# Attention block: queries and keys transposed by VectorE with transfers through DRAM, instead of by TensorE

## The chip, the core and the metric

The program runs on one NeuronCore of one Trainium2 chip. Its engines work in parallel, each through its own list of instructions in order: TensorE (PE, matrix products; PEld is its weight load), VectorE (DVE), ScalarE (ACT), GpSimd (POOL) and SyncE (SP), which here only issues transfers (DMA). TensorE writes into PSUM, eight banks of 128 x 512 fp32 words; everything else lies in SBUF. The metric is device time in microseconds (us) of one execution, lower being better. Where several runs were taken, their median is given.

## The reference

All data are fp32. One transformer block with its layernorms behind the additions:

```python
x = layernorm(x + attn(x));  x = layernorm(x + ffn(x))     # x: (2, 512, 512)

def attn(x):                       # 32 query heads, 8 key/value heads, 128 wide
    q = rmsnorm(heads(x @ Wq.T), q_norm_w)
    k = rmsnorm(heads(x @ Wk.T), k_norm_w)
    v = heads(x @ Wv.T)
    scores = einsum('bkgqd,bksd->bkgqs', grouped(q), k) / sqrt(128)
    bias = where(rel > 0, -1e30, slopes * rel)   # causal, ALiBi: one slope per query head
    return merge(softmax(scores + bias) @ v) @ Wo.T

def ffn(x):                        # inner width 1376, integer weights with a scale per row
    return ((silu(x @ gate.T * gs) * (x @ up.T * us)) @ down.T) * ds
```

`rmsnorm` divides each head's 128 numbers by their root mean square and multiplies by a weight of 128 numbers.

## The kernel before

**Order of the work.** The kernel doesn't issue instructions as it describes them. `Work.add` records each operation with what it reads and writes, a priority and a cost estimate per engine that could run it. `emit` then goes through a planned time: of all operations that are ready and have room in their buffers, the one that can start earliest goes next, ties by priority. The result is one fixed instruction list per engine. Where two engines are allowed (ScalarE or VectorE for an eviction, say), the plan also chooses. Buffers come from rings (`Ring`): so many slots each, taken when the first operation on a buffer is placed, free again when its last one is planned to have ended.

**Attention.** There are 8 groups (a key/value head with its 4 query heads), 2 batches and 4 blocks of 128 tokens: 64 units (g, b, i), run two at a time as 32 pairs. Groups 0 to 5 go through both batches in turn; the last two groups go through batch 0 and then batch 1, so (7, 1) is the last group and batch. For each pair:

- `project` (L759) makes q, k and v of both blocks with a Strassen-like scheme of seven products (`seven`, L605, its matmuls at L617) into `c`, a ring of 2 slots. The first pair uses plain products (L733).
- `heads` (L827) squares q and k (ScalarE, L842), sums (VectorE, L851), takes the power -1/2 (GpSimd, L544) and multiplies into `sq` (L558), a single buffer. GpSimd or ScalarE copies v out of `c` into `v`, and half a block of it into `vs` (L892 to L911). Then TensorE transposes the four query heads of each block into the PSUM bank `ptq` (L920), and an eviction with the weight as its scale brings them to `qT` (L928 on ScalarE, L930 on VectorE), a ring of 2. The keys of both blocks go the same way through `ptk` (L943) to `kT` (L950, L952). Both use the one slot of the PSUM ring `pt`.
- `scores` (L964): 4 matmuls per unit, each of 32 tokens x 4 heads against up to 512 keys (L979). VectorE adds the bias and takes the maximum (L988), ScalarE takes the exponential with its sum (L1004), and ScalarE or GpSimd divides (L1036, L1038), giving the probabilities `pr`.
- `attend` (L1050): every block of 128 keys of `pr` is turned without TensorE. VectorE transposes 32 x 32 squares into `st` (L1072). SyncE stores `st` to `far` in DRAM (L1081), and two loads bring it back in the wanted order as `prT` (L1092). Then TensorE multiplies with v (L1115) and an eviction gives `aT`. `st` and `prT` share a ring of 8 slots. Units 1 and 3 take half a block more along; what is left over for two units is done in one go (`halves`, L1143).
- For groups 0 to 5 `project_out` (L1215) multiplies with Wo by two levels of seven products (`inner`, L1327, matmuls at L1338); groups 6 and 7 use `project_pair` (L1296). VectorE adds everything into `acc`.

Weights for the next group are loaded beside the work: `w` (L402) and `wo` (L449), a ring of 1, whose load waits until the old one has been used.

**The rest.** Layernorm (`norm1`, L1477), the feed-forward part (`ffn_up`, L1631; `ffn_down`, L1795) and the last layernorm with the stores. It runs from some 760 us on.

**Queues.** All transfers but six go through SyncE's queue, in the plan's order. An instruction that waits there holds back everything behind it. Each transfer uses one of eight semaphores in turn.

Of the kernel before, what the change touches and what calls it, by code (L numbers as in the profile page):

```python
# [38 lines left out]
MAX_INIT = 3e38  # L39
DEEP = HKV - 2  # L40
# [15 lines left out]
def act(n, scaled=False):  # L56
    return 0.15 + 0.00084 * n + (0.1 if scaled else 0.0)
# [18 lines left out]
class Ring:  # L76
# [12 lines left out]
    def room(self):  # L89

        best = None
        if self.pool is not None:
            for k, b in enumerate(self.slots):
                t = 0.0
                for u in b.users if b else ():
                    if u["end"] is None:
                        break
                    t = max(t, u["end"] + LAG[u["eng"]])
                else:
                    if best is None or t < best[0]:  # L100
                        best = (t, self, k)
        if self.later is not None:
            found = self.later.room()
            if found is not None and (best is None or found[0] < best[0]):
                best = found
        return best
# [21 lines left out]
class Work:  # L128
# [51 lines left out]
    def emit(self):  # L180
# [23 lines left out]
        def room(o):  # L204

            t = o["at"]
            for b in o["takes"]:
                if b.tile is not None:
                    continue
                r = b.ring  # L210
                found = r.room()
                if found is None:
                    return None
                t = max(t, found[0])
            return t
# [56 lines left out]
def post_ln_block(  # L272
# [4 lines left out]

# [31 lines left out]
    def ring(stage, name, bufs, shape, dtype=F32):  # L309
        r = Ring(name, bufs, shape, dtype)  # L310
        rings.setdefault(stage, []).append(r)
        return r
# [6 lines left out]
    r_pt = ring("psum", "pt", 1, [P, S])  # L319
    r_po = ring("psum", "po", 1, [P, S])  # L320
# [6 lines left out]
    r_qw = ring("all", "qw", 1, [P, HKV])  # L327
    r_kw = ring("all", "kw", 1, [P, 1])
# [14 lines left out]
    r_c = ring("qkv", "c", 2, [P, 2, 2, W3])  # L343
# [7 lines left out]
    r_qT = ring("att", "qT", 2, [P, 2, G * Q, 2])  # L351
# [108 lines left out]
    def idle(e):  # L460
# [3 lines left out]
    warm = Buf(r_pt, "warm")  # L464
    W.add({"PE": 2.9}, -9.0, idle, [A(ident)], [A(warm)])
    load_qkv(0, -9.0)
    load(0.01, -8.9, lambda q: q.dma_start(qw[:, 0:1], qnw), [A(qw)])
    load(0.01, -8.9, lambda q: q.dma_start(kw.tile, knw), [A(kw)])
    W.add(
        {"DVE": 0.1},  # L470
        -5.0,
        lambda e: nc.vector.tensor_scalar_mul(kw.tile, kw.tile, math.sqrt(HD)),
        [A(kw)],
        [A(kw)],
    )
# [3 lines left out]
    for g in reversed(range(1, HKV)):  # L479
        W.add(  # L480
            {"DVE": 0.1},
            -5.0,
            lambda e, g=g: nc.vector.tensor_scalar_mul(
                qw[:, g : g + 1], qw[:, 0:1], SHRINK**g
            ),
            [A(qw)],
            [A(qw)],
        )
# [337 lines left out]

    def heads(p, prio):  # L827
# [52 lines left out]
        for r in range(2):  # L880
            tensor(
                5 * HD,
                prio,
                lambda r=r: sq[:, r],
                lambda r=r: c(r)[:, : 5 * HD].rearrange("p (h d) -> p h d", h=G + 1),
                lambda r=r: inv[:, r].unsqueeze(2).to_broadcast([P, G + 1, HD]),
                ALU.mult,
                [(cb, (r, 0)), (cb, (r, 1)), (inv, r)],
                [(sq, r)],
            )  # L890
            copy_op(
                HD,  # L892
                prio + 0.2,
                lambda r=r: v[:, i + r, :],
                lambda r=r: c(r)[:, 5 * HD :],
                [(cb, (r, 1))],
                [(v, i + r)],
                ("ACT", "POOL"),
            )

        v2 = Buf(r_vs, f"vs_{p}")
        v2s[p] = v2
        copy_op(
            HD,
            prio + 0.2,
            lambda: v2[P // 2 :, :],
            lambda: c(0)[: P // 2, 5 * HD :],
            [(cb, (0, 1))],
            [A(v2)],
            ("ACT", "POOL"),  # L910
        )  # L911
        for r in range(2):
            key = f"{g}_{b}_{i + r}"
            pt = Buf(r_pt, f"ptq_{key}")
            qT = Buf(r_qT, f"qT_{key}")
            qTs[g, b, i + r] = qT

            def transposes(e, r=r, pt=pt):
                for h, k in enumerate((0, 1, 3, 4)):
                    nc.tensor.transpose(pt[:, ts(h, P)], sq[:, r, k, :], ident.tile)  # L920

            W.add({"PE": 4 * TR}, prio + 0.4, transposes, [(sq, r), A(ident)], [A(pt)])

            def evict(e, pt=pt, qT=qT):
                src = pt.tile.rearrange("p (h m c) -> p m h c", h=G, m=2)
                dst = qT.tile.rearrange("p m (h r) k -> p m h (r k)", h=G)
                if e == "ACT":
                    nc.scalar.activation(dst, src, AF.Copy, scale=qw[:, g : g + 1])  # L928
                else:
                    nc.vector.tensor_scalar_mul(dst, src, qw[:, g : g + 1])  # L930

            W.add(
                {"ACT": act(S, True), "DVE": dve(S) + 0.05},
                prio + 0.4,
                evict,
                [A(pt), A(qw)],
                [A(qT)],
            )
        ptk = Buf(r_pt, f"ptk_{p}")

        def transposes_k(e):
            for r in range(2):
                nc.tensor.transpose(ptk[:, ts(r, P)], sq[:, r, 2, :], ident.tile)  # L943

        W.add({"PE": 2 * TR}, prio + 0.4, transposes_k, [(sq, 0), (sq, 1), A(ident)], [A(ptk)])
        def evict_k(e):
            dst = kT[:, i * P : (i + 2) * P].rearrange("p (m k r) -> p m k r", m=4, k=2)
            src = ptk[:, : 2 * P].rearrange("p (m r k) -> p m k r", m=4, k=2)
            if e == "ACT":
                nc.scalar.activation(dst, src, AF.Copy, scale=kw.tile)  # L950
            else:
                nc.vector.tensor_scalar_mul(dst, src, kw.tile)  # L952

        W.add(
            {"DVE": 0.48, "ACT": act(2 * P, True)},
            prio + 0.4,
            evict_k,
            [A(ptk), A(kw)],
# [5 lines left out]
    def scores(u, prio):  # L964
# [8 lines left out]
        for a in range(NQ):  # L973
# [6 lines left out]
                    sc[:, :w], lhsT=qT[:, a // 2, :, a % 2], rhs=kT[:, :w], start=True, stop=True  # L980
# [69 lines left out]
    def attend(u, prio):  # L1050
# [9 lines left out]
        for j in range(i + 1):  # L1060
            st, prT = Buf(r_prT, f"st_{key}_{j}"), Buf(r_prT, f"prT_{key}_{j}")
            prTs[u, j] = prT
            a0 = 2 if j == i and r == 0 else 0
            reads = [(pr, a) for a in range(a0, NQ)]
            if j == i and r:
                reads += [(pr, ("x", a)) for a in range(2)]

            n = (NQ - a0) * Q
            far = Buf(r_far, f"far_{key}_{j}")

            def squares(e, j=j, st=st, a0=a0, n=n):
                nc.vector.transpose(  # L1072
                    st[:, : NQ * n].rearrange("p (m a q) -> p a m q", m=NQ, q=Q),
                    pr[:, a0:, ts(j, P)].rearrange("p a (m k) -> p a m k", m=NQ),
                )

            W.add({"DVE": dve(NQ * n)}, prio, squares, reads, [A(st)])
            load(
                0.26 * n / P,
                prio + 0.1,  # L1080
                lambda q, st=st, far=far, n=n: q.dma_start(  # L1081
                    far[: P * NQ * n].rearrange("(m p c) -> p m c", m=2, p=P),
                    st[:, : NQ * n].rearrange("p (m c) -> p m c", m=2),
                ),
                [A(far)],
                [A(st)],
            )
            for m in range(2):
                load(
                    0.13 * n / P,  # L1090
                    prio + 0.1,
                    lambda q, m=m, far=far, prT=prT, n=n: q.dma_start(  # L1092
                        prT[ts(m, H2), : G * n].rearrange("p (h c) -> p h c", h=G),
                        far[m * H2 * NQ * n : (m + 1) * H2 * NQ * n].rearrange(
                            "(h k c) -> k h c", h=G, k=H2
                        ),
                    ),
                    [(prT, m)],
                    [A(far)],
                )  # L1100
# [8 lines left out]
        for j in range(i + 1):  # L1109
# [13 lines left out]
                [(prT, 0), (prT, 1), (v, j)] + ([A(po)] if j else []),  # L1123
# [16 lines left out]
        banks = (Buf(r_pt, f"px_{key}"), Buf(r_po, f"pz_{key}"))  # L1140
# [17 lines left out]
        for q, j in both:  # L1158
            reads += [(prTs[(g, b, j), j], m) for m in range(2)] + [(v, j), A(v2s[q])]
# [317 lines left out]
    def norm1(t, prio):  # L1477
        b, i = divmod(t, NTB)
        layernorm(t, prio, lambda: y_row(t), y_keys(t), f"a{t}")
        pt = Buf(r_pt, f"ptx_{t}")  # L1480
# [314 lines left out]
    def ffn_down(t, prio):  # L1795
# [37 lines left out]
        for r in (0, 1):  # L1833
            bank = Buf(r_pt, f"ps_{t + r}")
# [105 lines left out]
```

## Time and profile before

| | us |
|---|---|
| median of 3 runs | 999.28 (996.18 to 1000.93) |
| profiled execution, its own time | 998.64 |
| span of that execution in the trace | 996.9 |
| granted TensorE clock in it | 0.995 |

| engine | busy us | share of the span | instructions |
|---|---|---|---|
| TensorE, matmuls | 976.9 | 98% | 4538 |
| TensorE, weight loads | 712.9 | 72% | 4538 |
| VectorE | 722.8 | 73% | 1743 |
| GpSimd | 495.9 | 50% | 573 |
| ScalarE | 451.0 | 45% | 1184 |

DMA moved 119.78 MB in 160267 packets. SyncE's queue issued 592 transfers.

How to read it: a matmul of fp32 shows as two records, a transpose as one. Matmuls are pipelined, so one record lasts from its start until its result has come out, and the next one starts before that. What a matmul takes out of TensorE's time is therefore the distance from its start to the next start. Idle time stands in the profile with the instruction that ended the wait. Idle time of an engine that is not the bottleneck costs nothing.

### The profile page before, as it was taken

To read this page: it belongs to the slowest core of one execution; us is meant where nothing else is said; L and a number is where in the kernel's file an instruction comes from. 1 tells how busy PE (TensorE), PEld (TensorE's weight loads), DVE (VectorE), ACT (ScalarE), POOL (GpSimd) and SP (SyncE) were. 2 spreads that over 40 slices of the span, in tenths; PEclk is the share of its full clock that TensorE was granted. 3 is DMA by queue.
4 is the path that set the end of the run, shared out by engine and by line. 5 is a ranking of instruction groups with operands and counts; after the bars stand their busy time and mean duration, and the time that the engine had idled before them with its cause. 6 is when DMAs were issued, how large, how long until landed. Compare 5 with 4: busy or idle time off the path is not lost. (4 is left out here: it accounts for less than half of the span.)

```text
span 996.9 us, 14270 instructions
## 1 busy us (share of the span) xinstructions
PE 976.9 (98%) x4538; PEld 712.9 (72%) x4538; DVE 722.8 (73%) x1743; ACT 451.0 (45%) x1184; POOL 495.9 (50%) x573
## 2 busy tenths in 40 slices
PE   9999999999999999999999999999989999999997
PEld 5566776577767767676767676776747688888886
DVE  7877676877877888778767888776776586668544
ACT  2756354555355545645564445444454333433100
POOL 6774384537444646654567387565434152123120
PEclk9999999999999999999999999999999999999999
DMA  8273336425414634262436263725256443210001
GB/s 313 79 209 112 105 110 183 130 85 159 138 43 148 190 107 126 77 194 91 143 88 208 77 206 94 215 60 149 75 170 172 112 117 85 80 51 22 12 31 43
DMA packets 160267, 119.78 MB, mean 120 GB/s; under 512 B 27488, under 2 KB 151008, under 8 KB 158912
## 3 DMA queue, kind: packets, MB, share of 16 engines
q1 hardware_dynamic: 159328, 118.21, 39.5%
q8 instruction: 36, 0.59, 0.3%
q10 hardware_dynamic: 864, 0.66, 0.2%
q14 instruction: 39, 0.32, 0.1%
HBM read 78.98 MB, written 39.85 MB: 119 GB/s over the span
## 5 line engine op out<-in xcount | busy, mean ns | idle before, releaser
L1004 ACT ACTIVATE pr<-pr,nmax 128x32 f32<-128x32 f32 (+15 forms) x256 | 131.4, 514 | 69.2 <-DVE nmax L988 68.2
L979 PE MATMUL sc<-kT,qT 128*128 128x160 f32 (+15 forms) x512 | 149.6, 405 | 1.5 <-DVE nmax L988 1.4
L1115 PE MATMUL pa<-prT,v 128*128 128x512 f32 (+1 forms) x320 | 139.4, 518 | 5.4 <-DMA prT<-far 5.3
L988 DVE CUSTOM_DVE_ANT_0 pr<-sc,bias 128x32 f32<-128x32 f32 (+15 forms) x256 | 108.4, 434 | 36.5 <-PE sc L979 33.3
L979 PEld LDWEIGHTS sc<-kT,qT 128*128 128x128 f32 x512 | 89.7, 196 | 43.2 <-issue 21.2
L558 DVE TENSOR_TENSOR acc<-acc,pa_o 128x512 f32<-128x512 f32 (+2 forms) x128 | 72.8, 569 | 50.7 <-PE pa_o L1338 33.5
L1072 DVE STREAM_TRANSPOSE st<-pr 128x512 f32<-128x512 f32 (+1 forms) x160 | 96.0, 635 | 3.8 <-ACT pr L1036 2.1
L1036 ACT ACTIVATE pr<-pr,rden 128x64 f32<-128x64 f32 (+12 forms) x204 | 85.5, 481 | 26.5 <-DVE rden L1019 26.1
L617 PE MATMUL pa_q<-tq,sx 128*128 128x384 f32 x248 | 90.8, 489 | 0.0
L1038 POOL TENSOR_SCALAR pr<-pr,rden 128x256 f32<-128x256 f32 (+12 forms) x84 | 41.9, 508 | 75.3 <-DVE rden L1019 74.6
L714 ACT COPY c<-pa_q 128x384 f32<-128x384 f32 x84 | 39.9, 476 | 87.0 <-PE pa_q L617 83.9
L1115 PEld LDWEIGHTS pa<-prT,v 128*128 128x128 f32 x320 | 54.6, 193 | 24.8 <-issue 7.1
L714 ACT COPY gu<-pa_h 128x256 f32<-128x256 f32 (+1 forms) x88 | 32.3, 370 | 76.1 <-PE pa_h L617 62.1
L544 POOL TENSOR_TENSOR inv<-ms,nhalf 128x10 f32<-128x10 f32 (+1 forms) x33 | 64.0, 1939 | 4.3 <-DVE ms L865 2.8
L617 PEld LDWEIGHTS pa_q<-tq,sx 128*128 128x128 f32 x248 | 45.2, 190 | 27.6 <-issue 5.2
L851 DVE TENSOR_REDUCE ms<-sq 128x5 f32<-128x640 f32 x64 | 51.4, 813 | 7.7 <-ACT sq L842 7.7
L928 ACT ACTIVATE qT<-ptq,qw 128x512 f32<-128x512 f32 x50 | 34.3, 687 | 49.8 <-PE ptq L920 49.6
L842 ACT ACTIVATE sq<-c 128x640 f32<-128x640 f32 x64 | 45.6, 731 | 23.6 <-DVE c L558 21.5
L558 POOL TENSOR_TENSOR sq<-c,inv 128x640 f32<-128x640 f32 x42 | 52.7, 1267 | 0.6
L714 ACT COPY aT<-pa 128x512 f32<-128x512 f32 (+1 forms) x48 | 25.1, 522 | 51.4 <-PE pa L1115 50.7
L558 DVE TENSOR_TENSOR c<-pb_q,c 128x384 f32<-128x384 f32 x62 | 34.1, 550 | 19.6 <-PE pb_q L617 14.4
L617 PE MATMUL pa_h<-tx,sw 128*128 128x256 f32 (+1 forms) x176 | 46.1, 386 | 2.2 <-ACT gu L714 2.2
(226 smaller groups left out, 2233.5 us busy)
## 6 DMA issues: line engine op xcount, KB each, us to landing
far<-st SPq DMA_DIRECT2D x128, 256.0 KB, 2.3
prT<-far SPq DMA_DIRECT2D x256, 128.0 KB, 3.0
w<-in_wqkv_dram SPq DMA_DIRECT2D x39, 384.0 KB, 5.1
wo<-in_wot_dram SPq DMA_DIRECT2D x10, 1024.0 KB, 5.1
far<-st SPq DMA_DIRECT2D x32, 128.0 KB, 1.9
prT<-far SPq DMA_DIRECT2D x64, 64.0 KB, 2.4
wi<-in_gwt_dram SPq DMA_DIRECT2D x14, 256.0 KB, 3.0
wi<-in_uwt_dram SPq DMA_DIRECT2D x14, 256.0 KB, 3.4
```

The lines of the kernel that those rows point to most:

```text
L544: lambda e: nc.gpsimd.tensor_tensor(dst(), src(), nhalf[:, :n], ALU.pow),
L558: lambda e: vec[e].tensor_tensor(dst(), a(), b(), alu),
L617: nc.tensor.matmul(bank[:rows, :width], lhsT=a(fa, c), rhs=b(fb, c), start=(fresh and c == 0), stop=(c == depth - 1), skip_group_check=True,)
L714: nc.scalar.copy(dst(), src())
L842: lambda e, r=r: nc.scalar.activation(sq[:, r].rearrange("p h d -> p (h d)"), c(r)[:, : 5 * HD], AF.Square),
L851: lambda e, r=r: nc.vector.tensor_reduce(ms[:, r], sq[:, r], AX.X, ALU.add),
L979: lambda e, a=a, w=w, sc=sc: nc.tensor.matmul(sc[:, :w], lhsT=qT[:, a // 2, :, a % 2], rhs=kT[:, :w], start=True, stop=True),
L988: lambda e, a=a, w=w, sc=sc: nc.vector.tensor_tensor_reduce(out=pr[:, a, :w], in0=sc[:, :w], in1=bias[:, S - w :], scale=-(SHRINK**-g), sc ...
L1004: lambda e, a=a, w=w: nc.scalar.activation(pr[:, a, :w], pr[:, a, :w], AF.Exp, bias=nmax[:, a : a + 1], scale=-1.0, accum_out=den[:, a : a ...
L1036: nc.scalar.activation(dst, src, AF.Copy, scale=rden[:, a : a + 1])
L1072: nc.vector.transpose(st[:, : NQ * n].rearrange("p (m a q) -> p a m q", m=NQ, q=Q), pr[:, a0:, ts(j, P)].rearrange("p a (m k) -> p a m k", ...
L1115: lambda e, j=j, prT=prT, n=n: nc.tensor.matmul(by_head(po.tile)[:, :, P - n // G :], lhsT=v[:, j, :], rhs=late(prT, j, n), start=(j == 0) ...
```

## The change

- `NEAR_Q` and `NEAR_P` name two pairs of group and batch, (0, 0) and (7, 1), "near" from here on; the other 14 are "far".
- Queries and keys of the far ones (28 pairs): VectorE transposes the 32 x 32 squares (`squares`), SyncE stores the result to DRAM (`far_away`) and a load with another order of the blocks brings it back as `qT`, or as `raw` for the keys. The keys are multiplied with the weight on the way to `kT` (`weigh`, ScalarE or GpSimd). In the near ones TensorE transposes as before.
- The probabilities of the near ones go to TensorE: up to four transposes per block into a PSUM bank, and an eviction to `prT`. The far ones are unchanged but for the helper functions.
- v and vs of the far ones: four and two transfers from `c`, straight into the order of rows that the products want, in place of copies by ScalarE and GpSimd.
- The weights of the query norm and of the key norm are multiplied together once per group and applied to the keys alone; queries have no scale any more.
- Rings: `c` 2 to 3, `qT` 2 to 3; the PSUM rings `pt` and `po`, one bank each, become one ring `po` of two. `st` and `raw` of queries and keys come from the ring of `prT`. `room` now counts each slot only once if an operation takes two buffers of one ring.
- Layouts on the host: tokens in their natural order, the heads as q, k, v. `sc` reads `qT[:, a, :]` in place of `qT[:, a // 2, :, a % 2]`.

```diff
+NEAR_Q = {(0, 0), (HKV - 1, 1)}
+NEAR_P = {(0, 0), (HKV - 1, 1)}
...
-    r_pt = ring("psum", "pt", 1, [P, S])
-    r_po = ring("psum", "po", 1, [P, S])
+    r_po = ring("psum", "po", 2, [P, S])
...
-    r_c = ring("qkv", "c", 2, [P, 2, 2, W3])
+    r_c = ring("qkv", "c", 3, [P, 2, 2, W3])
...
-    r_qT = ring("att", "qT", 2, [P, 2, G * Q, 2])
+    r_qT = ring("att", "qT", 3, [P, NQ, P])
...
+    def squares(st, dst, src, n, prio, reads):
+        W.add(
+            {"DVE": dve(n)}, prio, lambda e: nc.vector.transpose(dst(), src()), reads, [A(st)]
+        )
+
+    def far_away(st, n, parts, name, prio):
+        far = Buf(r_far, f"far_{name}")
+        load(
+            0.26 * n / S,
+            prio,
+            lambda q: q.dma_start(
+                far[: P * n].rearrange("(m p c) -> p m c", m=parts, p=P),
+                st[:, :n].rearrange("p (m c) -> p m c", m=parts),
+            ),
+            [A(far)],
+            [A(st)],
+        )
+        return far
...
+        if (g, b) in NEAR_P:
...
+        else:
+            for m in range(NQ):
+                at = H2 * (m // 2) + m % 2
+                load(
+                    0.13 / NQ,
+                    prio + 0.2,
+                    lambda q, m=m, at=at: q.dma_start(
+                        v[at : at + H2 - 1 : 2, i : i + 2, :], cb[ts(m, Q), :, 1, 2 * HD :]
+                    ),
+                    [(v, (i + r, m)) for r in range(2)],
+                    [(cb, (r, 1)) for r in range(2)],
+                )
+            for m in range(2):
+                load(
+                    0.02,
+                    prio + 0.2,
+                    lambda q, m=m: q.dma_start(v2[H2 + m : P : 2, :], cb[ts(m, Q), 0, 1, 2 * HD :]),
+                    [(v2, m)],
+                    [(cb, (0, 1))],
+                )
...
         for r in range(2):
             key = f"{g}_{b}_{i + r}"
-            pt = Buf(r_pt, f"ptq_{key}")
-            qT = Buf(r_qT, f"qT_{key}")
+            st, qT = Buf(r_prT, f"sq_{key}"), Buf(r_qT, f"qT_{key}")
             qTs[g, b, i + r] = qT
-
-            def transposes(e, r=r, pt=pt):
-                for h, k in enumerate((0, 1, 3, 4)):
-                    nc.tensor.transpose(pt[:, ts(h, P)], sq[:, r, k, :], ident.tile)
...
+            squares(
+                st,
+                lambda st=st: st.tile.rearrange("p (m h q) -> p h m q", m=NQ, h=G),
+                lambda r=r: sq[:, r, :G, :].rearrange("p h (m d) -> p h m d", m=NQ),
+                G * HD,
+                prio + 0.3,
+                [(sq, r)],
+            )
+            there = far_away(st, S, 1, f"q_{key}", prio + 0.3)
+            load(
+                0.26,
+                prio + 0.3,
+                lambda q, qT=qT, there=there: q.dma_start(
+                    qT.tile, there.tile.rearrange("(a d c) -> d a c", a=NQ, c=P)
+                ),
                 [A(qT)],
+                [A(there)],
+            )
+        st, raw = Buf(r_prT, f"sk_{p}"), Buf(r_prT, f"raw_{p}")
...
+        there = far_away(st, 2 * P, 1, f"k_{p}", prio + 0.3)
+        load(
+            0.13,
+            prio + 0.3,
+            lambda q: q.dma_start(
+                raw[:, : 2 * P].rearrange("p (a c) -> p a c", a=NQ),
+                there[: 2 * P * P].rearrange("(a d c) -> d a c", a=NQ, c=2 * Q),
+            ),
+            [A(raw)],
+            [A(there)],
+        )
...
+            if (g, b) in NEAR_P:
+                pt = Buf(r_po, f"pt_{key}_{j}")
+
+                def transposes(e, j=j, pt=pt, a0=a0):
+                    for a in range(a0, NQ):
+                        nc.tensor.transpose(pt[:, ts(a - a0, P)], pr[:, a, ts(j, P)], ident.tile)
+
+                W.add({"PE": (NQ - a0) * TR}, prio, transposes, reads + [A(ident)], [A(pt)])
+                copy_op(
+                    NQ * n,
+                    prio,
+                    lambda prT=prT, n=n: prT[:, : G * n].rearrange("p (h a q) -> p a h q", h=G, q=Q),
+                    lambda pt=pt, n=n: pt[:, : G * n].rearrange("p (a h q) -> p a h q", h=G, q=Q),
+                    [A(pt)],
+                    [(prT, 0), (prT, 1)],
+                )
+                continue
```

## The prediction

> **What bounds the kernel now.** I first read the busy time by stretches, split where the attention part ends.
>
> ```profile
> core 0: us, PE busy (x) PEld busy (x) DVE busy (x) ACT busy (x) POOL busy (x), PEclk, DMA share, GB/s
> 0.00:760.00 760.00, 748.52 (x3515) 522.40 (x3516) 578.60 (x1430) 388.85 (x1045) 437.02 (x502) 1.00 0.46 137
> 760.00:997.00 237.00, 228.37 (x1024) 190.48 (x1022) 144.25 (x313) 62.15 (x139) 58.84 (x71) 0.99 0.22 66
> ```
>
> TensorE works 748.5 of the first 760 us; VectorE, next, 578.6 (76%). So in the part that the change touches only two things count: what TensorE has to execute, and whether its work arrives in time. A busy share can hide overlap, so I asked the timeline what transposes take out of TensorE's stream.
>
> ```profile
> 388.32 0.61 PE L1338 MATMUL pb_o<-wo,si 128*128 128x128 f32 x4
> 388.76 0.60 PE L920 MATMUL ptq<-ident,sq 128*128 128x128 f32 x4
> 389.20 0.49 PE L617 MATMUL pc_q<-w,xT 128*128 128x384 f32 x1
> ```
>
> Four transposes start at 388.76 and the next matmul starts at 389.20: 0.44 us, 0.110 us each. The 275 ns in the groups below is one transpose with its pipeline tail, which overlaps the next; multiplying by it would overstate the gain 2.5 times.
>
> ```profile
> L920 PE MATMUL ptq<-ident,sq 128*128 128x128 f32 x256 | 38.9, 275 | 0.1
> L943 PE MATMUL ptk<-ident,sq 128*128 128x128 f32 x64 | 12.5, 275 | 1.3 <-DVE qT L930 0.8 <-ACT qT L928 0.3
> L1072 DVE STREAM_TRANSPOSE st<-pr 128x512 f32<-128x512 f32 x128 | 83.0, 684 | 3.5 <-ACT pr L1036 2.1 <-POOL pr L1038 1.3 <-DMA far<-st 0.2
> L1072 DVE STREAM_TRANSPOSE st<-pr 128x256 f32<-128x256 f32 x32 | 14.0, 438 | 0.3 <-POOL pr L1038 0.2
> ```
>
> The last two rows are what VectorE pays when it turns a block instead. Next, what TensorE already waits for where values come round through DRAM (the waits: total, times, longest), and how long a transfer takes to land (issue groups):
>
> ```profile
> PE pa L1115 <- DMA prT<-far: 5.3, 8, 1.8
> PE ptk L943 <- DVE qT L930: 0.8, 1, 0.8
> PE ptk L943 <- ACT qT L928: 0.3, 1, 0.3
> ```
>
> ```profile
> far<-st SPq DMA_DIRECT2D x128, 256.0 KB, 2.3
> prT<-far SPq DMA_DIRECT2D x256, 128.0 KB, 3.0
> prT<-far SPq DMA_DIRECT2D x64, 64.0 KB, 2.4
> xT<-in_xt_dram SPq DMA_DIRECT2D x3, 512.0 KB, 6.3
> ```
>
> The 160 round trips of the probabilities cost TensorE 5.3 us in all, 33 ns each: a trip of over 5 us is nearly always covered.
>
> **The change, part by part.** (1) *Transposes taken from TensorE.* Far pairs are 28 of 32, with 8 query and 2 key transposes each: 280 x 0.110 = 30.8 us less.
>
> (2) *Transposes given to TensorE.* In the two near group-and-batches the probabilities return to it: the order of the built, unrun kernel has 72, so 7.9 us more. Net -22.9 us of a stream that is otherwise unbroken. The waits for the one bank ptq and ptk shared (0.8 + 0.3 us) go with them in nearly all pairs: -1.0.
>
> (3) *Latency of queries and keys.* Before: 0.44 us of transposes and a 0.69 us eviction. Now: VectorE 0.68, store 2.3, load of qT. No row shows that load (256 KB in 512-byte runs). It lies between prT's 3.0 (128 KB, same runs) and xT's 6.3 (512 KB); I take 3.5, near prT. Keys add a weighing, 0.47 as in the present eviction by ScalarE. So about 6.5 us against 1.1, or 10 at the slow end. What covers it is in the order of TensorE: I counted the matmuls between a pair's last projection and its first score, at their columns (four of 384 columns take 1.29 us in the chain). For the 28 far pairs that is 22.4 us on average before, 14.0 at least; after, 33.6 and 18.7, because a third c buffer and a third qT let projections run ahead. The cover grows by 11 us where the need grows by 5.4 to 9. The other steps from projection to sq are the same on both sides: addition 0.55, squares 2 x 0.73, sums 2 x 0.81, power with its addition 2.25, product 1.27, 7.2 us in all. The least cover, 18.7, exceeds 7.2 + 6.5, and also 7.2 + 10. The blocks on their way (st, sk, raw) also take slots of the prT ring, 14 a pair where 10 were; its 8 slots are for some 24 us per pair, 192 slot-us, and at 5 to 10 us each 14 take 70 to 140. Without cover, the excess would come at every pair: 28 x 5.4 = 151 us. So I charge the known rate: three new trips per far pair, 84, less 20 of the near probabilities, 64 x 33 ns = +2.1; bounds 0 and four times that, 8.4.
>
> (4) *SyncE's queue.* Twelve transfers per far pair, 336, less 60: 276 on top of 592. Issuing takes 0.37 us (far) to 0.61 (prT), so 100 to 170 us more on a queue now near 300 (160 x 0.37 + 320 x 0.61 + some 110 x 0.43) of 760: at most 63%. The queue keeps order, so whatever waits holds back what stands behind:
>
> ```profile
> SPq L449 <- PE pb_o L617: 17.8, 2, 13.3
> ```
>
> Here the load of wo waited for TensorE to leave the old one. A query block behind such a wait is late; behind it stand prT, v, raw and qT, and the scores and products wait for those. The least cover in (3) leaves 18.7 - 13.7 = 5.0 us, so the longest of the two waits, 13.3, could show as 8.3 and the clock's 1.7 of (7); the other, 4.5, would not. Taken as 0, since most pairs have 15 us more cover, bounds 0 to 10. The values' six transfers per pair (32 KB and less, under prT's 2.4 us) replace copies on ScalarE and GpSimd; first used only at the products after scores and softmax, so nothing at present waits for them.
>
> (5) *Transfer volume.* Added 56 x 512 KB + 28 x 256 KB + 28 x 160 KB = 40 MB, less 9 MB near: 31 on the 104 MB of the first 760 us (137 GB/s). The share goes from 0.46 to about 0.62. No bound.
>
> (6) *VectorE.* Added 56 x 0.684 + 28 x 0.438 = 50.6, and 5 near evictions at 0.69 (the copy of aT of that size), 3.5. Removed: 14 query evictions at 0.749, 7 key evictions at 0.482, near blocks 16 x 0.684 + 4 x 0.438: 26.6. Net +27.5: 606 of about 737 us, 82%. ScalarE loses 50 x 0.687 + 25 x 0.475 in evictions and 13 in copies, 59 us, and gets some 24 back (19 weighings, 14 blocks of probabilities and 7 of queries). Cost of VectorE taken as 0, bounds 0 to 27.5.
>
> (7) *The end of attention.* The last group and batch is near, and there the waits for prT gather:
>
> ```profile
> 735.33 1.08 PE L979 MATMUL sc<-kT,qT 128*128 128x224 f32 x4 [0.49 <-DVE nmax L988]
> 738.17 1.98 PE L1115 MATMUL pa<-prT,v 128*128 128x512 f32 x2 [1.75 <-DMA prT<-far]
> ```
>
> ```profile
> 730.00:740.00 10.00, 6.39 (x17) 2.98 (x18) 7.85 (x24) 6.05 (x20) 4.62 (x8) 0.91 0.77 237
> 740.00:750.00 10.00, 10.00 (x45) 6.95 (x44) 6.36 (x18) 3.80 (x9) 2.46 (x4) 0.92 0.65 175
> ```
>
> After the 1.75 us wait the granted clock averages 0.91 and 0.92 over two 10 us stretches: 0.9 + 0.8 = 1.7 us lost besides. With 0.65 and 0.27 shortly before, 4.4 us belong to the trip through DRAM, which near blocks don't make. I take half, -2.2 (bounds 0 and -4.4). At that rate, 1.7 of clock for 5.3 of waits, the new waits in (3) cost another 0.7.
>
> The Trainium skill ("VectorE: DVE Perf Modes", Rules for kernel authors) speaks against the change: it gives a 128x128 transpose to TensorE when PSUM will do as destination, as it does here. Its section The three transpose paths lists 390 ns for TensorE (bf16); at that price 208 transposes fewer would be worth 81 us, while the trace's 0.110 us, which counts here, makes 22.9.
>
> Sum against the profiled execution (998.6 us, span 996.9; the median shown is 999.3, 0.7 more): 998.6 - 22.9 - 1.0 + 2.1 + 0.7 - 2.2 = 975.3. Forecast 975 us, own range 966 to 985.
>
> **Rivals.**
> *VectorE gives part of it back.* It evicts TensorE's banks, and its densest 20 us now (320 to 340) has 16.4 busy; a pair's extra 1 us per 20 makes 87%. Against it: TensorE waits only 1.4 us for VectorE's maxima in the whole span, and ScalarE is relieved. If a third of 27.5 shows, 975 + 9 = 984.
>
> *Late queries: slower.* At the first scores of a far unit TensorE stands until qT has landed, held up in SyncE's queue as in (4). Each stall is priced as the one at 738: 1.75 + 1.7 of clock = 3.45 us. For it: the 13.3 us wait and transfers of 7 us seen among prT's slowest. Against: 33 ns per trip and the longer cover. It decides from 7 stalls among 56 far units (23.9 / 3.45). At one unit in four, 14: 998.6 - 23.9 + 48.3 = 1023.
> By the Trainium skill ("TensorE: Matmul & The Clock Gate", HAM oscillation) only idle gaps beyond about 3.4 us should bring the clock down; then each stall would cost 1.75 and 14 would be the turning point, but here the clock fell after 1.75.
>
> *Nothing gained.* Just those 7 stalls, or the bounds of (3) and (4), 6.3 and 10 more, with 9 of VectorE: 975 + 25 = 1000.
>
> **How the numbers follow.** Chances: forecast 0.70, VectorE 0.14, nothing 0.06, late queries 0.10. About 0.5% (5 us) is what a measurement of this kernel can tell from no change. Faster takes the first two less a little, 0.81; same 0.07; slower 0.12. Low end: 998.6 - 22.9 and all 11.5 us of idle time before 760 gone: 964. High end: 975 with the upper bound of waits (+6) and a little under half of VectorE's: 993.
>
> **What would show it.** ptq and ptk together near 40, 72 transposes of pt, at unchanged length; TensorE busy near 954; its waits for qT or kT under 3 us, for prT in the last 60 us of attention nearly none; PEclk 0.99 or more; VectorE near 750. It is wrong if TensorE's waits for qT, raw or v reach 10 us, if the clock falls in the middle of the span, or if VectorE passes 85% before the last attention.

## The result, and the profile after

| | before | after |
|---|---|---|
| median, taken together on one chip, us | 997.15 (993.66 to 1000.93, 20 runs) | 1005.62 (997.04 to 1013.48, 20 runs) |
| profiled execution, us | 998.64 | 1002.26 |
| its span, us | 996.9 | 1000.5 |
| granted TensorE clock in it | 0.995 | 0.994 |

The ratio is 1.0076, 95% interval 1.0054 to 1.0098: the change makes the kernel 0.8% slower, where the forecast was 975 us. First the busy time by stretches, columns as before:

```profile
0.00:760.00 760.00, 724.75 (x3248) 492.43 (x3249) 588.90 (x1447) 363.99 (x992) 439.66 (x467) 0.99 0.61 182
...
200.00:300.00 100.00, 90.43 (x391) 60.75 (x390) 76.25 (x180) 43.90 (x122) 49.09 (x50) 0.97 0.58 171
300.00:400.00 100.00, 92.59 (x430) 62.56 (x428) 76.27 (x188) 46.52 (x126) 56.67 (x57) 0.98 0.65 193
...
600.00:700.00 100.00, 90.62 (x428) 62.16 (x427) 77.19 (x183) 42.42 (x119) 57.70 (x60) 1.00 0.58 174
...
700.00:760.00 60.00, 58.96 (x259) 42.08 (x258) 46.44 (x138) 35.39 (x97) 39.11 (x48) 1.00 0.50 148
```

Of the first 760 us TensorE now works 724.8, where it worked 748.5. In three stretches of 100 us it stands idle for 7 to 10 us (before, the same stretches had 98.9, 99.9 and 99.7 us of work). VectorE's 588.9 are 77% of the 760, the transfers' share is 0.61. The groups that answer to those of before, and TensorE's waits (total, times, longest):

```profile
L968 PE MATMUL ptq<-ident,sq 128*128 128x128 f32 x32 | 4.8, 273 | 0.0
...
L983 PE MATMUL ptk<-ident,sq 128*128 128x128 f32 x8 | 1.5, 273 | 0.0
...
L1174 PE MATMUL pt<-ident,pr 128*128 128x128 f32 x72 | 10.5, 273 | 0.1
...
L834 DVE STREAM_TRANSPOSE sq<-sq 128x512 f32<-128x512 f32 x56 | 38.1, 688 | 2.1 <-ACT kT L1051 0.8 <-POOL sq L558 0.6 <-issue 0.5
```

```profile
PE pa L1223 <- DMA prT<-far: 16.9, 15, 2.6
PE pa_o L1447 <- DVE acc L558: 5.8, 2, 3.3
PE sc L1080 <- POOL kT L1053: 3.1, 2, 2.2
PE sc L1080 <- DMA qT<-far_q: 2.5, 2, 1.8
PE sc L1080 <- ACT kT L1051: 1.6, 1, 1.6
```

The transposes went as counted: 40 and 72. What grew is the wait for `prT`, from 5.3 to 16.9 us: the probabilities' own trips, which the change doesn't touch. There are fewer of them (140 for 160). Their loads land as long after the issue as before, 3.0 us; their stores a little later, 2.7 for 2.3:

```profile
far<-st SPq DMA_DIRECT2D x112, 256.0 KB, 2.7
qT<-far_q SPq DMA_DIRECT2D x56, 256.0 KB, 3.5
```

Matching every block's transpose, store, loads and product in the two traces says where the time goes. From the end of the transpose to the issue of the store it was 0.35 us on average and is now 1.39; from the store's landing to the first load's issue, 0.73 and now 1.09. In both stretches the data are there and SyncE hasn't issued the transfer yet; together they grew by 1.4 us, more than the store's 0.4. Landed less than 0.3 us before TensorE wanted them: 11 blocks of 160 before, 35 of 140 now. SyncE's timeline around one of the 15 waits (start, duration, line, transfer, how many), and the wait:

```profile
335.99 1.25 SPq L946 DMA_DIRECT2D v<-c  x2
337.34 1.60 SPq L843 DMA_DIRECT2D far<-st  x3
339.03 0.46 SPq L843 DMA_DIRECT2D far_k<-sk  x1
339.57 1.27 SPq L1200 DMA_DIRECT2D prT<-far  x2
340.94 0.55 SPq L843 DMA_DIRECT2D far_q<-sq  x1
341.58 2.57 SPq L1200 DMA_DIRECT2D prT<-far  x4
344.20 0.60 SPq L1039 DMA_DIRECT2D raw<-far_k  x1
344.90 0.45 SPq L843 DMA_DIRECT2D far_q<-sq  x1
345.45 0.38 SPq L1020 DMA_DIRECT2D qT<-far_q  x1
...
345.25 1.17 PE L1223 MATMUL pa<-prT,v 128*128 128x512 f32 x2 [2.60 <-DMA prT<-far]
```

Sixteen transfers go out back to back in 9.84 us, 0.62 us each; over the whole trace, the median step of transfers that follow without a pause is 0.64 us. The planner, `emit`, reckons SyncE free again 0.45 us after each (`free[e] = s + 0.45`), 7.2 us for sixteen. The list of every engine was put in order for a queue that would have been through these sixteen 2.6 us earlier.

### The profile page after: what moved, and what is told of

Same layout as the page of the kernel before. It is cut to its first block, busy times and chain, and to the rows that moved or that the text cites. A ratio compares the mean times of both kernels' runs of the same rounds, so it can differ in the third digit from the quotient of the medians.

```text
span 1000.5 us, 14246 instructions
## 1 busy us (share of the span) xinstructions
PE 959.4 (96%) x4330; PEld 691.4 (69%) x4330; DVE 734.7 (73%) x1767; ACT 430.2 (43%) x1137; POOL 500.0 (50%) x540
## 2 busy tenths in 40 slices
DMA packets 212044, 151.65 MB, mean 152 GB/s; under 512 B 44192, under 2 KB 195616, under 8 KB 210688
## 4 chain that ended last, share of the span: by engine, by line
PE 79%; DMA 11%; SPq 5%; DVE 4%; issue 1%; ACT 0%; ACTq 0%; POOLq 0%; POOL 0%; DVEq 0%
PE pa_q L617 13%; PE pa L1223 10%; PE sc L1080 9%; PE pa_h L617 8%; DMA prT<-far 6%; PE pa_o L1447 6%; PE pb_q L617 5%; PE pb_h L617 4%; PE pa_d L617 3%; PE pc_q L617 3%; PE pb_o L1447 3%; PE pa_o L617 3%; SPq L946 2%; PE pc_h L617 2%; PE pb_d L617 2%; DMA far<-st 1%
## 5 line engine op out<-in xcount | busy, mean ns | idle before, releaser
L1080 PE MATMUL sc<-kT,qT 128*128 128x160 f32 (+15 forms) x512 | 152.0, 405 | 7.7 <-POOL kT L1053 3.1
L1223 PE MATMUL pa<-prT,v 128*128 128x512 f32 (+1 forms) x320 | 138.5, 518 | 17.7 <-DMA prT<-far 16.9
L1080 PEld LDWEIGHTS sc<-kT,qT 128*128 128x128 f32 x512 | 87.4, 191 | 55.0 <-issue 22.7
L1137 ACT ACTIVATE pr<-pr,rden 128x64 f32<-128x64 f32 (+12 forms) x213 | 90.5, 490 | 38.4 <-DVE rden L1120 38.3
L714 ACT COPY c<-pa_q 128x384 f32<-128x384 f32 x94 | 44.6, 477 | 130.9 <-PE pa_q L617 124.8
L834 DVE STREAM_TRANSPOSE st<-pr 128x512 f32<-128x512 f32 (+1 forms) x140 | 85.3, 638 | 8.6 <-DMA far_k<-sk 4.6
L1139 POOL TENSOR_SCALAR pr<-pr,rden 128x256 f32<-128x256 f32 (+12 forms) x75 | 35.4, 482 | 96.2 <-DVE rden L1120 85.7
L867 ACT ACTIVATE sq<-c 128x640 f32<-128x640 f32 x64 | 45.9, 731 | 30.1 <-DVE sq L834 26.2
L1447 PEld LDWEIGHTS pa_o<-ti,si 128*128 128x128 f32 x336 | 44.2, 195 | 13.4 <-DVE acc L558 6.5
L1447 PE MATMUL pa_o<-ti,si 128*128 128x128 f32 x336 | 46.4, 279 | 5.8 <-DVE acc L558 5.8
L716 POOL CAST wf<-wi 128x512 f32<-128x512 int32 (+1 forms) x13 | 8.6, 659 | 81.9 <-PE pa_h L617 36.8
```

The source lines that it names most:

```text
L714: nc.scalar.copy(dst(), src())
L834: {"DVE": dve(n)}, prio, lambda e: nc.vector.transpose(dst(), src()), reads, [A(st)]
L1080: lambda e, a=a, w=w, sc=sc: nc.tensor.matmul(sc[:, :w], lhsT=qT[:, a, :], rhs=kT[:, :w], start=True, stop=True),
L1137: nc.scalar.activation(dst, src, AF.Copy, scale=rden[:, a : a + 1])
L1223: lambda e, j=j, prT=prT, n=n: nc.tensor.matmul(by_head(po.tile)[:, :, P - n // G :], lhsT=v[:, j, :], rhs=late(prT, j, n), start=(j == 0) ...
L1447: nc.tensor.matmul(bank[:, ts(c, P)], lhsT=a(fa, c), rhs=b(fb, c), start=fresh and c == 0, stop=True, skip_group_check=True,)
```

## The experiments

Three theories stood at first. **Q**: SyncE's queue is late. **B**: the added bytes make transfers land later. **V**: VectorE's added work, and the order that the planner makes of it. Runs of "before" beside each experiment had medians of 995 to 997 us; the ratios are to those. In the edits shown, `...` stands for code left out.

**Half of the new transfers away** (e1_v_copied). The values are copied by ScalarE and GpSimd in every pair, in plain row order, so the rows of v don't match those of `prT`; 168 transfers fewer.

```diff
-        if (g, b) in NEAR_P:
+        if True:
```

> The changed kernel, but v and vs of all pairs copied by ScalarE or GpSimd as before, rows left in plain order, so that the products take wrong rows of v; 168 transfers of 16 to 32 KB fewer, 104 us less of issuing on SyncE. Theory Q (SyncE's queue is the new limit: 472 us of issuing, transfers held up in line, prT comes late): 980 to 988 us, TensorE waiting under 8 us for prT. Theory B (bytes: the transfers themselves land later, 152 MB instead of 120): v is 4.5 of the 31 MB added, so 1002 to 1006. Theory V (VectorE and the planned order, not the transfers): 1003 to 1008, ScalarE and GpSimd being busier.

Measured 999.06 us, ratio 1.0037 (1.0017 to 1.0057): 6.6 us less than the changed kernel, about a third of what Q asked. Waits for `prT` fell only to 13.0 us, and those for VectorE's `acc` rose from 5.8 to 10.8. No theory had it.

**The value transfers issued twice** (e2_v_twice), the second time to DRAM that nobody reads:

```diff
+            for m in range(NQ + 2):
+                load(..., lambda q: q.dma_start(dump[:, :n, :], cb[ts(m, Q), :n, 1, 2 * HD :]), ...)
```

> The changed kernel with the six value transfers of every far pair issued a second time into a scratch buffer in DRAM, 168 more transfers, 4.5 MB. Q: SyncE's issuing goes from 472 to some 575 us, TensorE's waits for prT from 17 to 35 us or more: 1018 to 1050. B: 1006 to 1010. V: 1003 to 1008.

Measured 1080.99 us, ratio 1.0842 (1.0821 to 1.0863):

```profile
PE pa L1236 <- DMA prT<-far: 60.2, 34, 8.7
```

168 small transfers that nobody waits for cost 75 us. Longer waits for `prT` are 43 of them; the mean granted clock, 0.971 for 0.994, takes some 25 more by my estimate (2.9% of 1078 us less 0.6% of 1000). B and V are far off; Q undershot.

**The value transfers alone, in the kernel before** (e3_before_v_moved; 192 of them in plain row order; the rest is that of before):

```diff
-            copy_op(HD, ..., lambda r=r: v[:, i + r, :], lambda r=r: c(r)[:, 5 * HD :], ...)
+        for m in range(NQ):
+            load(..., lambda q, m=m: q.dma_start(v[ts(m, Q), i : i + 2, :], cb[ts(m, Q), :, 1, 2 * HD :]), ...)
```

> The kernel before with one part of the change alone: v and vs by the same number of transfers (6 per pair, 192 in all), everything else as before. Q: issuing goes from 318 to some 430 us, below the changed kernel's 472, so part of its waits: 1001 to 1008. B: 997 to 999. V: 994 to 998, since ScalarE and GpSimd lose their copies.

Measured 1010.12 us, ratio 1.0132 (1.0112 to 1.0152): 13 us slower, above even Q's range. So this part of the change, taken alone and ordered at the old price of a transfer, is a loss; at other prices it wasn't measured.

**The planner's price for a transfer** (e4_issue_cost), from 0.45 to 0.62 us:

```diff
-                free[e] = s + 0.45
+                free[e] = s + 0.62
```

> The changed kernel with one number of the plan changed: an issue on SyncE is planned at 0.62 us instead of 0.45 (measured: 0.61 for prT, 0.64 for v, 0.48 for qT). Q in the form that the plan's order is wrong because it believes the queue to be faster than it is: 980 to 992, waits for prT under 10 us. Q in the form that the queue is simply full: 1000 to 1012, the waits moving into the plan. B and V: 1002 to 1008.

Measured 998.06 us, ratio 1.0018 (0.9998 to 1.0038); waits for `prT` 8.7 us. Better by 7.5 us with no work removed, though less than hoped.

**VectorE relieved** (e5_no_squares). In the changed kernel ScalarE copies the query and key squares without turning them, so the output is another:

```diff
-            squares(st, ...)          # nc.vector.transpose
+            plain(st, ...)            # nc.scalar.activation(..., AF.Copy)
```

> The changed kernel, with the 84 transposes of query and key squares on VectorE replaced by plain copies of the same size on ScalarE; so the queries and keys are not turned within their 32 x 32 squares and the output is another. All transfers stay. It takes about 50 us of work from VectorE and gives about as much to ScalarE. Q (SyncE's queue is late, VectorE has room): no change against the changed kernel, 1003 to 1007 us, waits for prT near 20 us. V (VectorE is too full: probabilities' squares and acc sums come late, and its operations are stretched beside GpSimd's): 992 to 999 us, TensorE's waits on VectorE's acc gone, waits for prT under 14 us.

Measured 1016.5 us, ratio 1.0186 (1.0161 to 1.0211). Slower by 11 us, where V wanted 7 to 14 less. VectorE worked 706 us in that profile, ScalarE 464, and TensorE waited 21.4 us for `prT`.

**Both edits together** (e6_no_squares_v_copied):

> The changed kernel with both edits: values copied by ScalarE and GpSimd in plain row order (as in e1_v_copied), and the query and key squares copied by ScalarE without a turn (as in e5_no_squares); the output is another in both. Q alone: as e1_v_copied, 996 to 1001 us. V alone: as e5_no_squares, 992 to 999 us. Q and V together explain the loss: 980 to 990 us, prT waits under 9 us. Neither (the length of the trips or TensorE's order itself): 997 us or more.

Measured 1002.5 us, ratio 1.0050 (1.0028 to 1.0071): no explanation by Q and V as they were put. It falls under the last case, neither of them.

**The added VectorE work alone, in the kernel before** (e7_before_squares):

```diff
+                W.add({"DVE": dve(...)}, prio + 0.3, lambda e: nc.vector.transpose(dst(), src()), ...)   # 84 times, read by nobody
```

> The kernel before with the 84 added VectorE transposes of queries and keys alone: their results are written to slots of the prT ring and read by nobody; TensorE's transposes, the evictions and all transfers stay as before. V: 1001 to 1012 us, with new waits of TensorE for prT or on VectorE. Q: within 2 us of before, 995 to 999 us, as SyncE's queue is that of before.

Measured 1007.47 us, ratio 1.0098 (1.0077 to 1.0120). V's forecast holds. But TensorE's largest waits (5.3 us in all for `sq`, 4.4 for `prT`) are small; the time is in the plan itself, whose end moves by as much, as the table below shows.

**The value transfers on another queue** (e8_v_on_act_queue): the 168 issued by ScalarE in the changed kernel.

```diff
-                load(0.13 / NQ, ..., q.dma_start(v[...], cb[...]), ...)
+                load(0.13 / NQ, ..., q.dma_start(v[...], cb[...]), ..., "ACTQ")
```

> The changed kernel with the 168 transfers of v and vs issued by ScalarE in place of SyncE, nothing else; ScalarE is reserved for them in the plan (some 100 us more work on it). Bytes and packets are those of the changed kernel. Q: SyncE's queue is that of e1_v_copied, so 996 to 1001 us, and less if the waits that the value transfers hold the queue with (20 us of vs behind pz) matter too; issuing time on SyncE near 365 us. B (volume, or the landing of more transfers): 1003 to 1008 us. V: 1003 to 1008 us. If ScalarE is held by its transfers instead: over 1008 us, with TensorE waiting on ScalarE.

Measured 1013.70 us, ratio 1.0175 (1.0143 to 1.0207): the time of the last case of the expectation, but not its sign. TensorE's waits on ScalarE are small (2.3 us in all for `c`, the largest), and those for `prT` stay at 18.3; the loss is already in the plan, whose end is 28.6 us later (table below). An issue holds ScalarE as long as SyncE:

```profile
L950 ACTq DMA_DIRECT2D v<-c x112: 608/613/1627, 50.2 to 697.8; - x112
```

These are nanoseconds, least, median and most. The Trainium skill ("DMA: Bandwidth & Descriptors", Issuing engines are not separate DMA queues) says that initiating on several engines saves only the sequencer's time, "which is usually small relative to the DMA itself". The row has 0.61 us of issuing for a median landing of 3.0 us: a fifth, and here not small.

**A fourth theory: P, the planner's prices.** After these eight I set each result beside the kernel's own planned end, the latest `o["end"]` in `emit`. It is no measurement; what counts is how far the chip falls behind it.

| kernel | SyncE's transfers | plan's end | measured | difference | wait for prT |
|---|---|---|---|---|---|
| before | 592 | 978.5 | 997.2 | 18.6 | 5.3 |
| 84 VectorE transposes added to before | 592 | 988.8 | 1007.5 | 18.6 | 4.4 |
| value transfers added to before | 784 | 982.8 | 1010.1 | 27.3 | 8.5 |
| **after** | 868 | 949.8 | 1005.6 | 55.8 | 16.9 |
| after, values copied | 700 | 958.9 | 999.1 | 40.1 | 13.0 |
| after, values twice | 1036 | 974.6 | 1081.0 | 106.4 | 60.2 |
| after, 0.62 us per transfer | 868 | 968.0 | 998.1 | 30.1 | 8.7 |
| after, no squares on VectorE | 868 | 961.6 | 1016.5 | 54.9 | 21.4 |
| after, no squares, values copied | 700 | 961.3 | 1002.5 | 41.2 | 15.2 |
| after, values on ScalarE's queue | 700 | 978.4 | 1013.7 | 35.3 | 18.3 |

The plan saw the gain: 28.7 us less for the changed kernel. The chip gave it back: the difference, the lag behind the plan, grew by 37.2. With the same SyncE queue it hardly moves (18.6 twice; 55.8 and 54.9; 40.1 and 41.2). Within each of the two kernels it grows with the transfers on that queue at the old price: 18.6 and 27.3 in the kernel before, 40.1, 55.8 and 106.4 in the changed one. Their number alone doesn't set it: 784 in the kernel before leave less (27.3) than 700 in the changed one (40.1), and no run shows why. The squares on VectorE belong to the other column: with or without them, what moves is the plan's end, +10.3 us in the kernel before (measured +10.6), and +11.8 when ScalarE takes them (measured +10.9). That is why V seemed right once and wrong once.

P says: let the planner know what a transfer costs, and the gain is there. For the numbers of the next expectations I kept each engine's list as it is and pushed back whatever waits, at the prices named ("replayed").

**The changed kernel with both prices raised** (e9_after_real_prices):

```diff
-                free[e] = s + 0.45
-                dma = max(dma, s + 1.6) + c
+                free[e] = s + 0.7
+                dma = max(dma, s + 1.9) + c
```

> The changed kernel with two prices of its planner put right: a transfer holds SyncE's queue for 0.70 us in the plan (0.45 as it is; the trace's median steps are 0.61 to 0.69), and the first byte lands after 1.9 us (1.6). The same work, in another order. P (prices: the order of all engines is written out for a queue faster than the real one, and all engines then wait in that order): the planner's own end was 949.8 us for the changed kernel and 978.5 for the one before; replaying the changed kernel's order at 0.70 and 1.9 ends at 1013.7, and an order made for these prices ends at 957.9: 955 to 978 us measured. Q (there are simply too many transfers): 992 to 1006 us, as e4_issue_cost or worse. V (VectorE, ScalarE and the rest): over 1000 us.

Measured 973.16 us (970.80 to 976.19), ratio 0.9782 (0.9759 to 0.9804). P holds, and the others are out.

**The kernel before with the same two prices** (e10_before_real_prices):

> The kernel before with the same two prices, 0.70 and 1.9 us. P: its order replayed at these prices ends at 1005, an order made for them at 980.5: 978 to 993 us, so that the change, both orders made with right prices, brings 15 to 25 us, the 22.7 us of TensorE's work that it saves. Q and V: no change, 994 to 999 us, as before had room on SyncE's queue.

Measured 995.76 us, ratio 1.0005 (0.9992 to 1.0018). No change, as Q said and P didn't: P's replay had put before at 1005 us, 8 over, and so promised a gain for which there was no room; the plan's end itself went from 978.5 to 980.5. The control does what it is for: the new prices don't make every kernel faster, and the one with 592 transfers gains nothing. With these prices on both sides it is 973.16 - 995.76 = -22.6 us.

**168 transfers fewer as well** (e11_fewer_transfers): queries and keys of a pair go out and come back in one trip, and `vs` is copied from `v`.

```diff
-            there = far_away(st, S, 1, f"q_{key}", prio + 0.3)
...
+        load(0.65, ..., lambda q: q.dma_start(far..., st.tile...), ...)      # queries and keys, 2 x 128 + 64 columns
+        load(0.65, ..., lambda q: q.dma_start(qk.tile, far.tile.rearrange("(a d c) -> d a c", ...)), ...)
...
+            copy_op(HD, prio + 0.2, lambda: v2[H2:, :], lambda: v[:H2, i, :], ...)
```

> The changed kernel with the two prices of e9_after_real_prices and 168 transfers fewer: queries and keys of a pair of tiles go out and come back in one trip (2 transfers of 640 KB in place of 6), and vs is copied from v by ScalarE or GpSimd in place of two transfers; the prT ring has 7 slots in place of 8 for want of room. The output is the reference's. P: the plan's end is 954.8 us, 3 us less than e9_after_real_prices: 952 to 975 us. Q: at least 15 us less than e9_after_real_prices. V: no better than e9_after_real_prices.

Measured 964.92 us, ratio 0.9710 (0.9691 to 0.9729): 8 us less than with the prices alone, inside P's range; Q wanted 15.

**One price alone** (e12_issue_price_alone): 0.70 us per transfer, the landing left at 1.6.

> The changed kernel with the step of SyncE's queue at 0.70 us in the plan and the landing left at 1.6 us: which of the two prices of e9_after_real_prices matters. The plan's end is 949.1 us; its order replayed at 0.70 and 1.9 ends at 958.3, against 957.9 for e9_after_real_prices and 1000.2 for e4_issue_cost (0.62). If the step is what matters: 968 to 980 us. If the landing: 985 to 1000 us. If e9_after_real_prices was a lucky order and prices are beside the point: anywhere from 975 to 1005 us, with waits for prT again over 10 us.

Measured 964.38 us (964.22 to 965.99), ratio 0.9687 (0.9670 to 0.9703): as fast as the run with 168 transfers fewer, with one constant of the changed kernel altered, and below every range written down. Its work is that of the changed kernel: 4330 matmul records, 151.65 MB. Its first 760 us and its waits for transfers:

```profile
0.00:760.00 760.00, 751.38 (x3426) 519.82 (x3426) 601.42 (x1488) 376.20 (x1009) 469.05 (x492) 1.00 0.61 184
```

```profile
PE pa L1223 <- DMA prT<-far: 1.7, 3, 1.1
PE sc L1080 <- DMA qT<-far_q: 0.7, 1, 0.7
```

TensorE works 751.4 of 760 us (724.8 in the changed kernel), beside a busier VectorE and as many bytes; the clock stays at 1.00. The waits for `prT` are 1.7 us for 16.9. Blocks that landed less than 0.3 us ahead are 12 of 140 (35 in the changed kernel, 4 with both prices). SyncE issues as much as before the edit, 455 us of the first 760 (451 in the changed kernel), and the queue is little quicker to serve the blocks: stores go out 0.89 us after the transpose (1.39 in the changed kernel), first loads 1.25 us after the store's landing (1.09), and the stores land after 3.0 us (2.7). What changed is when TensorE asks for the blocks, not how long they take. Transfers held up in line aren't the difference either: those of `vs` hold the queue for 22.7 us behind `pz` here, 20.1 in the changed kernel.

The four orders made with 0.70 us, in the sequence told, were planned to end at 957.9, 980.5, 954.8 and 949.1 us; the chip was 15.3, 15.3, 10.1 and 15.3 behind, where the changed kernel was 55.8 and with 0.62 us 30.1 behind. The replays at 0.70 and 1.9 us fall the same way: 1013.7, 1000.2 and 958.3 for the orders made with 0.45, 0.62 and 0.70 (measured 1005.6, 998.1 and 964.4). That the order made with 0.45 is what lost the time is shown by this and by the control; how much of it is another matter.

What stays open: 0.62 us gave 998 and 0.70 gave 964. Of these 34 us, 18.9 are the plan's own end (968.0 and 949.1): the planner takes what can start first, and small changes of a price move its end by some 10 to 20 us either way. Planned, not run, at steps from 0.40 to 0.80 us and both landings, the changed kernel ends between 949 and 990 us and the kernel before between 978 and 990; the changed kernel as it stands and the run above, 949.8 and 949.1, are the two earliest. So how much of the 964 is the price and how much a fortunate order is not settled, and the 22.6 us above hold for one pair of orders. Nor is it shown that the true price is what helps, rather than one with something to spare: 0.70 lies above the 0.62 and 0.64 us of the trace, and 0.62 left the chip 30.1 us behind. Other prices weren't measured.

## Why the prediction was wrong

**Steps (1) and (2), TensorE's work: right.** Adding up every matmul at the distance that its shape usually takes in an unbroken stretch at full clock gives some 23 us less after than before (22.7 to 23.3, by the distance taken as usual); 22.9 were forecast. The two profiled executions differ by +3.6, so the rest of TensorE's time, waits and slow clock, grew by some 26 to 27 us. By the waits of the trace, `prT` takes 11.6 more, `acc` 6.5 (5.8 shown above and 0.7 at the next product), `kT` and `qT` 7.2, and other waits 4 less: 21 in all. The clock was granted at half for 3.4 us at 206, 244 and 346 us, a sign of being wrong that the prediction had named.

**Step (4) is the one that failed**: "Taken as 0, since most pairs have 15 us more cover". Its share of the queue was right: at most 63% of 760 us were forecast for issuing, 59% came (451). It was put at 0 with bounds 0 to 10; the waits for `prT` alone grew by 11.6 and those for `kT` and `qT` by 7.2. The cover was reckoned for queries and keys alone. The probabilities stand in the same queue with much less to spare, and their store and loads are issued 1.0 and 0.4 us later than before. And a share of 59% says nothing of a dense stretch: sixteen transfers in one took 2.6 us more than planned. The runs put figures to it: the lag behind the plan grew by 37.2 us, 15.7 of it with the values' transfers (55.8 - 40.1), the rest (40.1 - 18.6) in the kernel that has the queries' and keys' trips without them. The price that was wrong, 0.45, stands in `emit`; the prediction had the measured 0.37 to 0.61 beside it, added them up to a share, and didn't ask what order the planner makes of its own figure.

**Step (3), the known rate: wrong with it.** The load of `qT` was well taken, 3.5 us. But 33 ns per trip belonged to the order of the kernel before. In the changed one a probability trip costs 16.9 / 140 = 121 ns, and `qT` and `kT` cost 7.2 us where under 3 were to show; with the order made for 0.70 us and the same 868 transfers it is 1.7 / 140 = 12 ns. The rival of late queries had the right queue but for the most part the wrong transfers: waits for `qT` are 2.5 us in all. The rival that comes nearest is "nothing gained", by its terms too: the upper bounds of (3) and (4), 18.4 us, and 9 of VectorE make its 1000 us. The profiled execution took 1002.3, with 18.8 us more waiting for `prT`, `kT` and `qT` and 6.5 for `acc`. The prediction gave it a chance of 0.06.

**Step (5): right** (0.61 for 0.62), and volume is no cause of the loss: the kernel at 964 us moves the same bytes, and its stores land later still (3.0 us for 2.7).

**Step (6), VectorE taken as 0: right for its load, not for its waits.** It worked 734.7 us (750 forecast), 77% of the attention part, and 601 us in the first 760 of the kernel at 964 us hardly held TensorE there. But the changed kernel has 6.5 us of waits for `acc`, and the two long ones (3.34 us at 242.7, 2.48 at 654.2) come right behind operations of VectorE that GpSimd had stretched, as told at the end: 4.06 us for two that take 0.41 each, and 4.77 for two that take 0.81 each. That the stretching causes these waits is likely, but no run separates it. No term had that.

**Step (7), the end of attention: right.** From 700 to 760 us TensorE works 58.96 at a clock of 1.00, where it had 56.18 at 0.97: 2.8 us for the 2.2 forecast, and of the waits for `prT` there 0.2 us are left (2.7 before).

The sum of the forecast, 975, is met within 2 us by the order made for 0.70 and 1.9 us (973.16). That closeness is partly luck, as orders made for nearby prices gave 998 and 964.

## What to carry to other kernels

Where a kernel writes out its own order by a cost model, check the model's prices against the trace before adding work of that kind: a price 0.2 us too low per transfer was nearly harmless at 592 transfers, and raising it brought 32 to 41 us at 868 (1005.6 against 973.2 and 964.4), a part of which may be a fortunate order. Look for the damage not on the added transfers but on those that already had the least to spare in the same queue. And set the planned end beside the measured one for every variant; the change in their difference tells an order that the chip can't keep from a change that doesn't pay.

## What the hardware showed besides

VectorE's additions and subtractions on SBUF data stretched fivefold when GpSimd worked beside them. Three of the same size in the changed kernel, and GpSimd's at that time:

```profile
235.28 2.03 DVE L558 TENSOR_TENSOR si<-aT 128x256 f32<-128x256 f32 x1
237.24 2.03 DVE L558 TENSOR_TENSOR aT<-aT 128x256 f32<-128x256 f32 x1
239.19 0.41 DVE L558 TENSOR_TENSOR si<-aT,si 128x256 f32<-128x256 f32 x1
...
234.89 2.14 POOL L558 TENSOR_TENSOR tq<-w 128x768 f32<-128x768 f32 x1
237.11 1.88 POOL L558 TENSOR_TENSOR tq<-w,tq 128x768 f32<-128x768 f32 x1
```

Each slow one ends 0.28 us after GpSimd's; the third, with GpSimd idle, takes 0.41 us. Operations at least 1.3 times as long as the shortest of their kind cost VectorE 5.5 us more in the first 760 us of the kernel before, 15.2 in the changed one, 17.3 with both prices raised and 11.0 at 964 us. So it comes with the change, whatever the prices, and isn't what the better orders won. The Trainium skill ("SBUF — State Buffer", SBUF: two separate sides) says that the loser of the pair's shared port waits for the whole of the other's instruction; these rows agree.

What a transfer's issue takes of SyncE doesn't go by its size: in the timeline above 0.62 us for the 32 KB of `v`, 0.64 for the 128 KB of `prT` and 0.38 for the 256 KB of `qT`.

The clock fell after other waits than the 1.75 us at the end of attention, too: from 200 to 210 us, where TensorE waited 2.19 us for `prT`, it averages 0.83. The length of a wait alone doesn't decide: in the changed kernel the clock fell after 2.19, 3.34 and 2.60 us (at 206, 244 and 346), and it stayed full after 2.48 us at 637.7 and again at 654.2.
